# A two-layer graph kernel: the PSUM bank of three extra transposes, the queue of the last row's store, and the order of one step of layer 0

## The chip, the cores and the metric

The kernel runs on one core of a Trainium2 chip. The metric is the device time of one execution in microseconds (us). A core has TensorE (PE, matmuls and transposes; its weight loads are listed as PEld), VectorE (DVE), ScalarE (ACT), GpSimd (POOL) and SyncE (SP). DMAs are issued from the queues of SP, ACT and POOL. Matmul results land in PSUM banks, which are handed out here as named tiles with a number of buffers each.

## The reference, cut to what matters

There are N = 4096 nodes with 512 features, and an adjacency of 4096 x 4096 int32 in which about one entry in a thousand is 1. Two layers follow each other, each with a residual and a layer norm.

```python
# layer 0: graph attention, 8 heads of 64
Wh = einsum('nf,hfo->hno', x, W)
f1 = Wh . a[:, :64];  f2 = Wh . a[:, 64:]
e = leaky_relu(f1[:, :, None] + f2[:, None, :], 0.2)
e = where(adj > 0, e, -9e15)
x = layernorm(x + softmax(e) @ Wh)
# layer 1: mean of the neighbours
agg = (adj > 0) @ x / max(deg, 1)
out = concat([x @ W_self + b_self, agg @ W_nb + b_nb]) @ W_comb + b_comb
x = layernorm(x + relu(out))
```

## The kernel before, in words

The kernel never multiplies by the adjacency. It reads it once, turns each row into a short list of neighbours, and then gathers only the listed rows. Rows are handled in 32 blocks of 128 (`NB`). `FB` is 4, the number of 128-wide pieces of the 512 features. `LB` is 30 and `EARLY` is 29.

**Adjacency stage (lines 907 to 947).** Each step `b` of the loop issues on SP the load of an x block (`load_x`) and of an adjacency block (`load_adj`, two halves of 1 MB in four buffers `at`). It then works on four things:

- *Lists.* `some(lists)` moves a generator on by one piece. These pieces (`decode` and its callers) are VectorE work of many small instructions, with some PE work, and they turn keys into indices and weights for groups of four blocks.
- *Transposes.* `transposed(w + 1)` transposes an x block on PE (L320) into a PSUM tile `tp`, of which there is one buffer. ScalarE copies it to `xT`. The column sums of x are taken on VectorE in even blocks (L330) and with ScalarE's four copies in odd ones (L333); for blocks from 29 on it does the copy alone (L326). Their sums are taken earlier: steps 22, 23 and 24 transpose blocks 29, 30 and 31 a first time with `only=True`, and only VectorE's sum (L330) reads that result. These are the extra transposes.
- *Masks.* `key_bank(b + 1)` and `mask_adj(b + 1, h)` run on ScalarE; a mask (L395) turns half an adjacency block into bf16, in three buffers `ab`.
- *Node block.* `node_block(w, xT, b)` computes one block of Wh with its attention terms in two halves: `node_half` is four products in PSUM (L341, tile `pw`, two buffers) and a VectorE copy into `row` (L345). Between the halves PE folds the masks into keys (`fold_adj`, L413) and VectorE takes their maxima (`max_keys`, L428). `node_rest` has small copies on VectorE and GpSimd. The block's row is stored in the table `t0` in HBM from GpSimd's queue (`store`, L905).

**Between the stages (lines 938 to 987).** The last node block is computed and stored, the last masks and folds run, and two weights of 1 MB each are loaded from SP's queue (`load_fold`, L252 and L253). `gather(t0, ...)` on GpSimd then issues five indirect DMAs for a block (L590), which read rows of `t0`, so they wait for all rows to be stored. In the meantime the weights of layer 1 are multiplied out (`fold_weights`, L269 and L281) and the last lists are decoded.

**Layer 0 (lines 995 to 1054).** The loop over `i` runs from -2 to 32 and is a software pipeline: one step touches blocks `i - 1` to `i + 4`. On PE the order of a steady step is `a_reach` (L657), `a_z` of block `i - 1` (L721, four products of 512 columns with the folded weight), the transposes of block `i` (L320) with the copy to `xT` on ScalarE and its store on SP (L729), `a_shared_sum` of block `i + 2` (L638, two products of 8 columns) and `a_shared` of block `i + 1` (L684, two products of 512 columns, added to the x block that ScalarE put into the PSUM tile `nm`). VectorE's L700 adds `nm` to the gathered sum `y`, ScalarE's `root` and `norm` (L708 to L716) finish the layer norm, and L716 writes the block that the transposes read. In step 0 there is no `a_z` yet.

**What sets the order.** The order of the instructions on each engine is the order of the program (`tc.manual_schedule()`, L791). Nothing is reordered afterwards. Tiles come from pools by name, and a tile taken again waits until the last reader of the buffer is done; semaphores carry these waits. Each engine takes its instructions in order, and so each DMA queue's issues stand in the instruction order of the engine that issues them.

Of the kernel before, what the change touches and what calls it, by code (L numbers as in the profile page):

```python
# [31 lines left out]
F32 = mybir.dt.float32  # L32
# [8 lines left out]
P = 128  # L41
# [49 lines left out]
def listed_layers(  # L91
# [15 lines left out]
    nc = tc.nc  # L107
# [3 lines left out]
    FB = FIN // P  # L111
# [23 lines left out]
    ps = ctx.enter_context(tc.tile_pool(name="ps", bufs=1, space=PSUM))  # L135
# [179 lines left out]

    def transposed(b, wp, sums=None, only=False):

        tp = ps.tile([P, FB, P], F32, name="tp", bufs=1)
        for c in range(FB):
            nc.tensor.transpose(tp[:, c, :], xs[:, b, ts(c, P)], ident)  # L320
        if only:
            t = tp
        else:
            t = wp.tile([P, FB, P], F32, name="xT", bufs=2)
        if sums is None or b >= EARLY and not only:
            nc.scalar.copy(t, tp)  # L326
        elif only or b % 2 == 0:
            if not only:
                nc.scalar.copy(t, tp)
            nc.vector.tensor_reduce(sums[:, :, b : b + 1], tp, AX.X, OP.add)  # L330
        else:
            for c in range(FB):
                nc.scalar.activation(  # L333
                    t[:, c, :], tp[:, c, :], AF.Copy, accum_out=sums[:, c, b : b + 1]
                )
        return t

    def node_half(b, k, xT, w_sb, row):
        pw = ps.tile([P, HW], F32, name="pw", bufs=2)
        for c in range(FB):  # L340
            nc.tensor.matmul(  # L341
                pw, lhsT=xT[:, c, :], rhs=w_sb[:, c, k * HW : (k + 1) * HW],
                start=(c == 0), stop=(c == FB - 1),
            )
        nc.vector.tensor_copy(row[:, k * HW : (k + 1) * HW], pw)  # L345

    def node_rest(b, row):
        nc.vector.tensor_copy(lst[:, b, KL + 3 :], row[:, TW:FW])
        nc.vector.tensor_reduce(  # L349
            fmax[:, b, 0:1], row[:, 0:H], AX.X, OP.max, apply_absolute_value=True  # L350
        )
        nc.gpsimd.tensor_copy(  # L352
            f1s[:, b, 0:K0, :], lst[:, b, KL + 3 :].unsqueeze(1).to_broadcast([P, K0, H])
        )
# [29 lines left out]
    def load_adj(b, ap):  # L384

        for h in range(NH):
            at = loads[b, h] = ap.tile([P, NG // NH, SC], I32, name="at", bufs=4)
            r = b * P + h * (P // NH)
            nc.sync.dma_start(
                at, adj[r : r + P // NH, :].rearrange("(j r) (s c) -> (r s) j c", r=RG, s=SEG)  # L390
            )

    def mask_adj(b, h):
        ab = masks[b, h] = bp.tile([P, NG // NH, SC], BF16, name="ab", bufs=3)
        nc.scalar.activation(  # L395
            ab, loads.pop((b, h)), AF.Relu, accum_out=asum[:, b, h : h + 1]
        )
# [9 lines left out]
    def fold_adj(b, dp):  # L407

        key = keys[b]
        ab = [masks.pop((b, h)) for h in range(NH)]  # L410
        for k in range(0 if b in FIRST else 1, 3):
            for t in range(P // 32):
                nc.tensor.matmul(  # L413
                    key[ts(t, 32), :],
                    lhsT=two if k == 0 else fold[:, k - 1, :],
                    rhs=cols if k == 0 else ab[t // 2][:, 2 * (t % 2) + k - 1, :],
                    start=(k == 0), stop=(k == 2), tile_position=(0, 32 * t),
                    skip_group_check=b not in FIRST,
                )
        if b % G == 0:  # L420
            kks[b // G] = dp.tile([P, G, 3, NC], F32, name="kk", bufs=2)

    def max_keys(b):

        kk = kks[b // G][:, b % G, 0, :]
        key = keys.pop(b)
        for q in range(4):
            nc.vector.max(kk[:, q * 8 : (q + 1) * 8], key[:, ts(q, P)])  # L428
# [177 lines left out]
    def gather_early(b, pool):  # L606
        return gather(t1[0 : 2 + min(LE + b, LX) * P, :], b, pool, idxe)
# [26 lines left out]
    def a_shared_sum(b):  # L634

        DN[b] = ps.tile([P, H], F32, name="sm", bufs=2)
        for k in range(KH):
            nc.tensor.matmul(  # L638
                DN[b], lhsT=OWN[b][:, k, :], rhs=E[b][:, K0 + k, :],
                start=(k == 0), stop=(k == KH - 1),  # L640
            )
# [28 lines left out]
    def a_weigh(b, sl, to=None):  # L670
        gv = G0[b][:, sl, H:TW].rearrange("p k (h d) -> p k h d", h=H)
        nc.vector.tensor_tensor(  # L672
            gv if to is None else to.rearrange("p (k h d) -> p k h d", k=1, h=H), gv,
            E[b][:, sl].unsqueeze(3).to_broadcast([P, sl.stop - sl.start, H, D]), OP.mult,
        )
# [6 lines left out]
    def a_shared(b):  # L682
        for k in range(KH):
            nc.tensor.matmul(  # L684
                NM[b], lhsT=OWN[b][:, k, :], rhs=G0[b][:, K0 + k, H:TW],
                start=False, stop=(k == KH - 1), skip_group_check=True,
            )

    def a_adds(b, wp):

        yp = ps.tile([P, HD], F32, name="pw", bufs=2)
        a_weigh(b, slice(0, 1), yp)
        a_weigh(b, slice(1, K0))
        nc.vector.tensor_add(yp, yp, G0[b][:, 1, H:TW])
        Y[b] = wp.tile([P, HD], F32, name="y", bufs=2)
        nc.vector.tensor_add(Y[b], yp, G0[b][:, 2, H:TW])
# [106 lines left out]
    def weight(pool, name):  # L803
        return pool.tile([P, FB, HD], F32, name=name)
# [47 lines left out]
    xT = transposed(0, wp, sums)  # L852
# [27 lines left out]
    bcol = bias_columns(brw)  # L880


    def node_block(w, xT, between=None):
        row = wp.tile([P, FW], F32, name="row", bufs=2)
        node_half(w, 0, xT, w_sb, row)
        if between is not None:
            fold_adj(between, dp)
            max_keys(between)
        node_half(w, 1, xT, w_sb, row)
        node_rest(w, row)  # L890
        store(w, row, nc.gpsimd)
        return row

    def on_own(b):
# [9 lines left out]
    def store(w, row, eng=nc.scalar):  # L904
        eng.dma_start(t0[2 + w * P : 2 + (w + 1) * P, :], row[:, 0:TW])  # L905

    w, lists = 0, []
    for b in range(LB - 1):
# [7 lines left out]
        for k in range(1 + (b in AHEAD)):  # L916
# [8 lines left out]
            w, xT = w + 1, nxt  # L925
# [10 lines left out]
        if b % G == G - 1:  # L936
            lists = [decode(b + 1 - G, dp, on_own)]
    load_adj(LB + 1, ap)
    node_block(w, xT)
    key_bank(LB)  # L940
    mask_adj(LB, 0)
    m2 = weight(fp, "wr")
    loaded = load_fold(1, w_nb, m2, weight(fc, "wc"))
    fold_adj(LB - 1, dp)
# [45 lines left out]
    def on(b):  # L990
        return 0 <= b < NB
# [3 lines left out]
    for i in range(-2, NB + 1):  # L995
        if on(i):
            a_moments(i)
        if on(i - 1 + GA):
            G0[i - 1 + GA] = gather(t0, i - 1 + GA, gps[(i - 1 + GA) % GA])
        elif i > 0:  # L1000
            b = i - 1 + GA - NB
            G1[b] = gather_early(b, gps[(NB + b) % GA])
        if on(i + 1):
            a_reach(i + 1)
        if i == -1:
            for k in range(2):
                next(m2s)
        if i >= -1 and on(i + 2):
            a_owned(i + 2, wq)
        if on(i + 1):  # L1010
            a_x(i + 1)
            a_normed(i + 1)
            a_weigh(i + 1, slice(K0, KS))
        if on(i + 2):
            a_weights(i + 2, wq)
        if on(i):
            root(i, xs[:, i, :])
        if on(i + 2):
            a_exp(i + 2)
        for k in range({-2: 3}.get(i, 0)):  # L1020
            some(lists)
        if on(i):
            norm(i, xs[:, i, :])
        if on(i - 1):
            a_z(i - 1, XT.pop(i - 1), m2, wp)
        if on(i + 1):
            a_adds(i + 1, wq)
        if on(i):
            XT[i] = transposed(i, wp)
            store_xT(i, XT[i])  # L1030
        if on(i + 2):
            a_shared_sum(i + 2)
            for k in range({-2: 1}.get(i, 0)):
                some(lists)
            a_sum(i + 2, wq)
            for k in range({-2: 1}.get(i, 0)):
                some(lists)
        for k in range({-2: 3, -1: 2}.get(i, 0)):
            next(m2s)
        if on(i + 1):  # L1040
            a_shared(i + 1)
        if on(i + 3):
            a_owners(i + 3, wp)
        if 2 <= i < 6:
            next(biased)
        if i == 7:
            loaded = load_fold(0, w_self, m1, weight(fc, "wc"))
        if 16 <= i < 20:
            if i == 16:
                biased = fold_bias(loaded, bcol[:, 0:FB])  # L1050
            next(biased)
        if i == 20:
            sum_bias()
# [14 lines left out]
    xT = load_xT(0, wp)  # L1068
# [10 lines left out]
    for b in range(2):  # L1079
        nxt = load_xT(b + 1, wp)  # L1080
        g_self(b, xT, m1)
        xT = nxt
# [23 lines left out]
    for b in range(NB):  # L1106
# [5 lines left out]
        if b + 2 < NB:  # L1112
            nxt = load_xT(b + 3, wp) if b + 3 < NB else None
            g_self(b + 2, xT, m1)
            xT = nxt
# [413 lines left out]
```

## Time and profile before

| | us |
|---|---|
| three timed runs | 694.48, 692.57, 690.92 (median 692.57) |
| the profiled execution, its own time | 690.14 |
| its span, first to last instruction | 688.4 |
| PE busy | 622.5 (90%), 2354 instructions |
| VectorE busy | 499.1 (72%) |
| ScalarE busy | 456.0 (66%) |
| GpSimd busy | 348.8 (51%) |
| mean granted TensorE clock | 0.966 |

The span in stages, from PE's timeline: the adjacency loop runs to 225, the stage between to 264, and layer 0's loop with layer 1 behind it takes the rest. All starts that are named in this document are in us from the first instruction of the profiled execution.

To read the lines below: an instruction's line has its start, its duration, the engine, the line of the code, the operation, the tiles (output<-inputs), the shapes and the number of instructions in the row; in brackets stands the time that the engine stood idle just before, and what ended that wait. "issue" is time in which the engine waited for nothing that the profile shows. In the slices, each digit is the busy share of a fortieth of the span in tenths, and PEclk is the granted clock of TensorE in tenths of full speed.

### The profile page before, as it was taken

What the parts mean: (1) busy time and instruction counts of PE and PEld (TensorE: products, weight loads), DVE (VectorE), ACT (ScalarE), POOL (GpSimd) and SP (SyncE); (2) the same over time, 40 slices, a digit from 0 to 9 for tenths busy, and PEclk for the clock granted to TensorE, in tenths of its full rate; (3) what the DMA queues carried; (4) which work ended last, traced back from release to release, by engine and by line L of the source; (5) the groups of instructions that cost most, each with busy time, mean ns of one, the idle gap of its engine ahead of it and who ended that gap; (6) DMA issues with size and microseconds to landing.
All of it is one profiled execution on the core that took longest, in us unless ns stands there. A gap on an engine that the chain in (4) does not pass through costs nothing.

```text
span 688.4 us, 9188 instructions
## 1 busy us (share of the span) xinstructions
PE 622.5 (90%) x2354; PEld 344.6 (50%) x2354; DVE 499.1 (72%) x1431; ACT 456.0 (66%) x1044; POOL 348.8 (51%) x411
## 2 busy tenths in 40 slices
PE   4798988987799597999999999999899999999993
PEld 2466766665567354545455445454344444444441
DVE  6237987998598787999998998897304666666663
ACT  3687988878487534767676767776316567767764
POOL 4011111110001477777677776746676677777760
PEclk9989999999899698999999999999999999999997
DMA  8999999999799877989989888868878899998992
GB/s 249 405 408 408 409 408 409 407 409 407 262 321 354 298 193 213 281 277 277 379 275 290 260 275 259 279 209 281 271 210 278 283 297 311 317 308 299 323 306 76
DMA packets 91974, 209.65 MB, mean 305 GB/s; under 512 B 13694, under 2 KB 13702, under 8 KB 91914
## 3 DMA queue, kind: packets, MB, share of 16 engines
q1 hardware_dynamic: 63024, 114.05, 44.8%
q0 software_dynamic: 28704, 94.66, 44.1%
q8 instruction: 21, 0.34, 0.2%
q14 instruction: 39, 0.32, 0.2%
q10 hardware_dynamic: 186, 0.28, 0.1%
HBM read 175.25 MB, written 33.69 MB: 304 GB/s over the span
## 4 chain that ended last, share of the span: by engine, by line
PE 56%; DVE 4%; DMA 4%; POOL 3%; issue 3%; ACT 2%; SPq 0%; DVEq 0%; POOLq 0%; ACTq 0%
PE pw L721 13%; PE nm L753 8%; PE pw L753 8%; PE nm L684 7%; PE nm L760 4%; PE pw L760 4%; POOL g L590 3%; PE tp L281 2%; PE tp L320 2%; PE pw L341 2%; PE sm L657 2%; DMA wc<-in_L_gnn_W_comb_dram 2%; PE sm L638 1%; DMA g<-t,idx 1%; DMA t<-row 1%
## 5 line engine op out<-in xcount | busy, mean ns | idle before, releaser
L590 POOL DMA_INDIRECT g<-t,idx x290 | 280.3, 967 | 109.1 <-issue 49.7
L395 ACT ACTIVATE ab<-at 128x2048 bf16<-128x2048 int32 x64 | 122.3, 1912 | 41.0 <-DMA at<-in_adj_dram 27.8
L341 PE MATMUL pw<-w_sb,xT 128*128 128x264 f32 x512 | 134.4, 409 | 7.0 <-issue 3.8
L721 PE MATMUL pw<-wr,xT 128*128 128x512 f32 x256 | 117.7, 603 | 0.7 <-ACT xT L326 0.7
L341 PEld LDWEIGHTS pw<-w_sb,xT 128*128 128x128 f32 x512 | 97.1, 199 | 36.0 <-issue 7.7
L352 POOL COPY f1s<-lst 128x24 f32<-128x24 f32 x32 | 7.8, 245 | 183.1 <-DVE fmax L349 100.5
L672 DVE TENSOR_TENSOR g<-g,key 128x1024 f32<-128x1024 f32 x64 | 77.9, 1217 | 1.1
L721 PEld LDWEIGHTS pw<-wr,xT 128*128 128x128 f32 x256 | 46.3, 191 | 47.2 <-issue 46.3
L684 PE MATMUL nm<-g,own 128*128 128x512 f32 x128 | 64.5, 627 | 0.0
L320 PE MATMUL tp<-ident,xs 128*128 128x128 f32 x268 | 44.9, 293 | 18.3 <-DVE sums L330 12.1
L753 PE MATMUL pw<-m,xT 128*128 128x512 f32 x128 | 57.6, 592 | 0.0
L753 PE MATMUL nm<-m,xT 128*128 128x512 f32 x128 | 57.6, 592 | 0.0
L320 PEld LDWEIGHTS tp<-ident,xs 128*128 128x128 f32 x268 | 32.3, 150 | 46.7 <-ACT xs L716 21.7
L707 ACT ACTIVATE xs<-y,ln_sum 128x512 f32<-128x512 f32 x32 | 23.1, 723 | 42.2 <-DVE y L700 40.2
L776 DVE SCALAR_TENSOR_TENSOR sm<-y,lst,nm 128x512 f32<-128x512 f32 x16 | 12.1, 756 | 52.9 <-PE nm L770 29.1
L345 DVE COPY row<-pw 128x264 f32<-128x264 f32 x64 | 26.9, 424 | 23.0 <-PE pw L341 17.4
L753 PEld LDWEIGHTS pw<-m,xT 128*128 128x128 f32 x128 | 24.4, 190 | 30.6 <-issue 30.3
L753 PEld LDWEIGHTS nm<-m,xT 128*128 128x128 f32 x128 | 24.4, 190 | 30.6 <-issue 30.6
L590 POOL DMA_INDIRECT g<-t,idxe x30 | 28.4, 947 | 18.2 <-issue 5.5
L281 PE MATMUL tp<-wc,row 128*128 128x512 f32 x64 | 30.9, 622 | 2.0 <-ACT m L285 1.2
L760 PE MATMUL nm<-g,own 128*128 128x512 f32 x64 | 30.2, 594 | 1.2 <-ACT nm L744 1.2
L684 PEld LDWEIGHTS nm<-g,own 128*128 128x128 f32 x128 | 22.5, 196 | 16.3 <-issue 15.6
(210 smaller groups left out, 1068.3 us busy)
## 6 DMA issues: line engine op xcount, KB each, us to landing
at<-in_adj_dram SPq DMA_DIRECT2D x64, 1024.0 KB, 10.7
t<-row POOLq DMA_DIRECT2D x32, 260.0 KB, 5.5
xt<-xT SPq DMA_DIRECT2D x32, 256.0 KB, 4.0
t<-row SPq DMA_DIRECT2D x32, 256.0 KB, 4.2
xT<-xt SPq DMA_DIRECT2D x32, 256.0 KB, 5.4
out_dram<-row SPq DMA_DIRECT2D x32, 256.0 KB, 5.2
xs<-in_x_dram SPq DMA_DIRECT2D x31, 256.0 KB, 10.9
g<-t,idx POOLq DMA_INDIRECT x290, 4.9
```

The source lines that it names most:

```text
L281: nc.tensor.matmul(mp, lhsT=wT[:, d, :], rhs=wc[:, d, :], start=(d == 0), stop=(d == FB - 1))
L320: nc.tensor.transpose(tp[:, c, :], xs[:, b, ts(c, P)], ident)
L341: nc.tensor.matmul(pw, lhsT=xT[:, c, :], rhs=w_sb[:, c, k * HW : (k + 1) * HW], start=(c == 0), stop=(c == FB - 1),)
L345: nc.vector.tensor_copy(row[:, k * HW : (k + 1) * HW], pw)
L395: nc.scalar.activation(ab, loads.pop((b, h)), AF.Relu, accum_out=asum[:, b, h : h + 1])
L590: nc.gpsimd.indirect_dma_start(out=out, out_offset=None, in_=table, in_offset=bass.IndirectOffsetOnAxis(ap=at, axis=0),)
L672: nc.vector.tensor_tensor(gv if to is None else to.rearrange("p (k h d) -> p k h d", k=1, h=H), gv, E[b][:, sl].unsqueeze(3).to_broadcast( ...
L684: nc.tensor.matmul(NM[b], lhsT=OWN[b][:, k, :], rhs=G0[b][:, K0 + k, H:TW], start=False, stop=(k == KH - 1), skip_group_check=True,)
L707: nc.scalar.activation(wide, Y[b], AF.Square, bias=MV[b], scale=-float(HD), accum_out=rs)
L721: nc.tensor.matmul(pz, lhsT=xT[:, c, :], rhs=m2[:, c, :], start=(c == 0), stop=(c == FB - 1))
L753: nc.tensor.matmul(NM[b], lhsT=xT[:, c, :], rhs=m1[:, c, :], start=False, stop=(c == FB - 1), skip_group_check=True,)
L760: nc.tensor.matmul(NM[b], lhsT=OWN[b][:, k, :], rhs=g[:, K0 + k, 0:HD], start=False, stop=(k == KH - 1), skip_group_check=True,)
```

## The change

Three edits are made together.

1. The extra transposes of steps 22 to 24 (`only=True`) are written to a buffer of the tile `pw`, the two banks that the halves of the node block use in turn. Before, they were written to the one bank `tp`, which all other transposes use.
2. The row of the last node block in the adjacency stage isn't stored from GpSimd's queue at the end of `node_block`. It is stored from ScalarE's queue, which issues it after `key_bank(LB)` and `mask_adj(LB, 0)`.
3. In step 0 of layer 0, `a_shared_sum(2)` and `a_shared(1)` are issued ahead of the transposes of block 0 and of what belongs to them (the copy to `xT`, and its store). In all other steps the order stays.

```diff
     def transposed(b, wp, sums=None, only=False):
 
-        tp = ps.tile([P, FB, P], F32, name="tp", bufs=1)
+        tp = ps.tile(
+            [P, FB, P], F32, name="pw" if only else "tp", bufs=2 if only else 1
+        )
...
-    def node_block(w, xT, between=None):
+    def node_block(w, xT, between=None, keep=False):
...
         node_rest(w, row)
-        store(w, row, nc.gpsimd)
+        if not keep:
+            store(w, row, nc.gpsimd)
         return row
...
     load_adj(LB + 1, ap)
-    node_block(w, xT)
+    row = node_block(w, xT, keep=True)
     key_bank(LB)
     mask_adj(LB, 0)
+    store(w, row)
     m2 = weight(fp, "wr")
...
         if on(i + 1):
             a_adds(i + 1, wq)
+        if i == 0:
+            a_shared_sum(i + 2)
+            a_shared(i + 1)
         if on(i):
             XT[i] = transposed(i, wp)
             store_xT(i, XT[i])
         if on(i + 2):
-            a_shared_sum(i + 2)
+            if i:
+                a_shared_sum(i + 2)
...
-        if on(i + 1):
+        if on(i + 1) and i:
             a_shared(i + 1)
```

`store` itself is unchanged. Its default queue is ScalarE's:

```python
    def store(w, row, eng=nc.scalar):
        eng.dma_start(t0[2 + w * P : 2 + (w + 1) * P, :], row[:, 0:TW])
```

## The prediction

> **What bounds the kernel now.** I read four views in this order: the slices of the span, to find a stage in which every engine is low at once; the timelines of the stage found, engine by engine; the chain of work that ended last, to see who sets the pace behind it; and the waits of the few lines that the edits touch.
>
> ```profile
> PE   4798988987799597999999999999899999999993
> ACT  3687988878487534767676767776316567767764
> PEclk9989999999899698999999999999999999999997
> DMA  8999999999799877989989888868878899998992
> ```
>
> A slice is 17.2 us. Slices 0 to 9 are the adjacency stage at its best: DMA at 9 and 408 GB/s. In slice 10 (172 to 189 us) PE falls to 7, ScalarE to 4 and DMA to 7, although adjacency rows are still to come. Asked by stretches, 175 to 185 us has PE busy 5.20 of 10 us at a clock of 0.66, and 185 to 195 us moves 141 GB/s. Nothing is the bound there: something waits. PE's timeline names it:
>
> ```profile
> 168.45 1.11 PE L320 MATMUL tp<-ident,xs 128*128 128x128 f32 x4 [1.23 <-ACT xT L333]
> ...
> 174.60 0.64 PE L320 MATMUL tp<-ident,xs 128*128 128x128 f32 x4
> 180.03 1.11 PE L320 MATMUL tp<-ident,xs 128*128 128x128 f32 x4 [4.80 <-DVE sums L330]
> 180.94 3.72 PE L341 MATMUL pw<-w_sb,xT 128*128 128x264 f32 x8
> 184.60 0.71 PE L413 MATMUL nm<-ab,fold 128*32 128x512 bf16 x8
> 185.23 2.05 PE L341 MATMUL pw<-w_sb,xT 128*128 128x264 f32 x8
> ...
> 190.69 0.66 PE L320 MATMUL tp<-ident,xs 128*128 128x128 f32 x4 [1.23 <-ACT xT L333]
> ```
>
> The second set of transposes in each of steps 22, 23 and 24 (168.45, 180.03, 190.69) is the extra one. It waits 1.23, 4.80 and 1.23 us for the one bank `tp`, since the first set must be read out of it. In step 23 that reader is VectorE:
>
> ```profile
> 179.29 0.68 DVE L330 TENSOR_REDUCE sums<-tp 128x4 f32<-128x512 f32 x1
> 181.18 0.69 DVE L330 TENSOR_REDUCE sums<-tp 128x4 f32<-128x512 f32 x1 [1.21 <-PE tp L320]
> ```
>
> VectorE reaches that sum only at 179.29, behind list work. Behind the stalled transposes on PE stand both Wh halves and the fold of step 23 (184.60), whose reading frees a mask buffer, so ScalarE stands too:
>
> ```profile
> 176.27 1.91 ACT L395 ACTIVATE ab<-at 128x2048 bf16<-128x2048 int32 x1
> ...
> 185.40 1.91 ACT L395 ACTIVATE ab<-at 128x2048 bf16<-128x2048 int32 x1 [7.12 <-issue]
> 224.85 1.91 ACT L395 ACTIVATE ab<-at 128x2048 bf16<-128x2048 int32 x1 [1.15 <-issue]
> ```
>
> After that PE sets the pace: 195 to 225 us has PE busy 29.91 of 30 us, and the chain runs through PE from there, then over masks, gathers and VectorE's decoding to layer 0, and through PE (L721, L684, L753, L760) to the end. So time saved before 195 us stays saved if nothing else comes late.
>
> **What the Trainium skill says.** "PSUM — Partial Sum Buffer", section "PSUM bank collisions raise a hardware error", asks for a semaphore guard by bank: a second writer of `tp` waits for the reader of all of it; the 4.80 us agree. Its section "Engine vs sequencer instructions" calls the queues of ScalarE, VectorE and GpSimdE strict FIFO: what stands behind a waiting issue waits too. "TensorE: Matmul & The Clock Gate", part 1, says that the clock is halved after an idle free-running window of about 3.4 us. The trace agrees, and is finer: asked window by window, PE busy 0.63 of 3.41 us (174.60 on) and 1.29 (263.35 on) are followed by a clock of 0.50; 1.68 (92.68 on) and 1.84 (51.72 on) aren't. "DMA: Bandwidth & Descriptors", section "Specifications", gives first bytes after about 1 us from GpSimd and 0.6 us from SP or ScalarE; here a 260 KB store from POOL lands after 5.5 us in the median, a 256 KB store from SP after 4.2.
>
> **The change, part by part.** All starts are of this execution.
>
> *Extra transposes in `pw`.* Three sets move, none is added: 4 x 0.13 us each. `pw` has two banks in rotation, so extra, half 0, half 1 now take three turns. The wait moves: half 1 takes the bank of the extra set and waits for its sum.
> Step 22: extra at 167.05; half 0 needs VectorE's copy of the half before (167.56 + 0.42), so 168.05 in place of 169.36. At half clock till 171.18 it ends at 171.5, where the fold now starts at 172.14: 0.64 us earlier. Half 1 needs the extra sum (170.37 + 0.66): no wait; 172.05 in place of 172.69.
> Step 23: VectorE copies half 1 at 174.0 to 174.43. First transposes 174.05, extra 174.55, half 0 at 175.05 (1.88 us), fold to 177.5. VectorE's list work between is unchanged: L478, at 175.39 now, to the sum at 179.29 is 3.90 us, so from 174.62 the sum is at 178.52, and the extra sum follows at once, to 179.80. Half 1 starts at 179.87 in place of 185.23: 5.36 us earlier, behind a new wait of 2.37 us. The mask at 185.40 moves to about 177.7.
> Step 24: the eight L493 products at 181.75, VectorE's L499 at 183.5 (now 189.02), and 4.48 us of its work later (189.02 to 193.50) the extra sum, 187.98 to 188.65. Half 1 at 188.7 in place of 193.60: **4.9 us earlier**, new wait 1.8 us. From here PE has no wait to 224, and I carry 4.9 us. DMA allows it: the load issued at 187.42 now goes out near 179.7 and, at 10.7 us to landing, is there at 190.4; its mask is at 199.03 - 4.9 = 194.1.
> The unknown is the clock: the new wait leaves PE busy about 1.55 us in the window from 178.01, between the 1.29 that halved it and the 1.68 that didn't. If it is halved, one window costs about 1.85 us. I take no halving and keep -3.05 as the other end.
>
> *Last Wh row from ScalarE.* POOL loses one issue (0.55 us). ScalarE gains one, between the masks that start at 221.71 and 224.85. It waits for the row's copy (DVE L345 at 224.26, 0.43), so until about 224.75; the three small stores of L246 to L248 took 0.24 to 0.28 us on ScalarE's queue, the x load 0.36. The mask behind it starts at 225.1 instead of 224.85; ScalarE then has no gap to 231.1, PE's last fold and VectorE's L428 at 232.36 wait for it: **+0.25 us**. The gathers gain but don't need it:
>
> ```profile
> 225.20 0.55 POOL L905 DMA_DIRECT2D t<-row  x1
> 232.54 1.05 POOL L590 DMA_INDIRECT g<-t,idx  x1 [6.79 <-PE sm L477]
> ```
>
> The releaser named isn't the cause: POOL's own wait before the first gather lasts 6.14 us from 225.3, and the store of 225.20 lands after 6.2. From ScalarE it lands 4.2 to 6.2 us after 224.75, so gathers start 0 to 2.5 us earlier, my value 2. But the first row's five gathers (fifth at 237.92) have landed by 242.7, at 4.8 us at most, and their first user is VectorE L628 at 250.84, which comes straight from list work. The cover is 8 us; the gain is 0, and a store landing up to 8 us late costs nothing either.
>
> *Shared product first in step 0.* Two L638 products and two L684 (eight passes) move ahead of four transposes on PE; the copy to xT and the store to xt (SP, empty then) move with them.
>
> ```profile
> 268.05 1.12 PE L320 MATMUL tp<-ident,xs 128*128 128x128 f32 x4 [3.41 <-ACT xs L716]
> 268.96 0.86 PE L638 MATMUL sm<-e,own 128*128 128x8 f32 x4
> 269.67 3.76 PE L684 MATMUL nm<-g,own 128*128 128x512 f32 x4
> ```
> ```profile
> 273.47 0.69 DVE L700 SCALAR_TENSOR_TENSOR y<-y,nm 128x512 f32<-128x512 f32 x1 [2.67 <-PE nm L684]
> ```
>
> L638 needs ScalarE's exp (267.06 + 0.24): 267.35. L684 then runs 268.0 to 271.7, VectorE's L700 1.75 us earlier, but the transposes end at 272.8 instead of 269.2. ScalarE is in order: the xT copy, owners, st and nm stand ahead of the next L707, which so starts at about 274.4, now 274.20. Its norm ends 2.93 us later, and PE's next transposes, at 277.28 now, don't move: **0**. If the shorter pause (2.7 us for 3.41) leaves the clock up, L684 takes 1.9 us, and the next transposes come at 274.9: -2.4 us. If the pause falls worse in its windows, I allow +1.
>
> Sum: -4.9 + 0.25 + 0 = -4.65 us on the profiled execution: 690.14 to 685.5 (its span is 688.4, 1.7 us lie around it). The three timed runs have a median of 692.57, 2.4 above it; the same difference on that gives **687.9**.
>
> **Rivals.**
> A, as worked out: 687.9, chance 0.42.
> B, the clock is halved in the new wait: -3.05 + 0.25 gives 689.8. For it: 1.55 us is nearer to unknown than to safe. 0.25.
> C, A and a full clock in step 0: 687.9 - 2.4 = 685.5. Against it: a pause of 2.7 us can still fill most of one window. 0.13.
> D, the bank change only renames the wait: if VectorE reaches the extra sum of step 23 near 185, half 1 stands as long as now, and 692.6 + 0.25 = 692.8. Against it: the sum waited 1.21 us for PE itself at 181.18, so it isn't VectorE that was late. 0.12.
> E, slower: the issue on ScalarE is held while the loads before it drain. Issues of x rows on SP, each behind two adjacency loads, took 0.33 to 5.04 us, 1.14 in the median; here 2 MB of weights are ahead, issued at 221.73 and 222.28, the second landing 13.0 us later, at 235.3. A hold until then, 10.5 us from 224.75, keeps the masks behind it: 692.6 - 4.9 + 10.5 = 698.2. It decides from a hold of 4.9 us. Against it: 0.24 us at 47 us, with DMA as full. 0.08.
>
> **How the numbers follow.** About 0.5%, 3.5 us, is what a measurement of this kernel can tell from no change: below 689.1 is faster, above 696.0 slower. The timed runs spread by 1.9 us around their median. Faster: 0.36 of A's 0.42, 0.09 of B, all of C: 0.58. Slower: most of E and, with the phase of the clock, a little of D; I give 0.07. Same: 0.35. The range goes from a little below C, 684.8, to D's middle, 692.5; outside lie E, half of D and the tail of C, under 0.2.
>
> **What would show it.** Right: no wait ahead of the extra transposes; waits near 2.4 and 1.8 us ahead of half 1 in steps 23 and 24, ended by the sums; no gap of 7 us on ScalarE; the fold of step 23 near 177, all PE starts around 200 to 220 near 4.9 us earlier; the store issue on ScalarE below 0.4 us; the first user of gathers without a wait for DMA; in step 0, L700 earlier but the next transposes not. Wrong: half 1 waiting 5 us or more; a clock of 0.50 in 181 to 185; a mask held by the store; a shift before 195 us that is gone by 225, which would mean that loads or masks, not PE, pace that stage.

## The result, and the profile after

The changed kernel takes 691.70 us in the median of 20 runs (688.04 to 694.32), the kernel before 692.85 us in the median of 20 (689.15 to 696.40). The ratio is 0.9973, with a 95% interval from 0.9956 to 0.9990: 1.9 us faster, with 0.7 and 3.0 us as ends (the two medians lie 1.15 us apart). The forecast was 4.65 us. In the runs below, all but those of first_4, bank_3, bank_sm_2 and sm_warm_2, every kernel, before among them, took 785 to 810 us in the median, because VectorE and ScalarE paused again and again behind 240 us, mostly for 7 to 15 us and for a reason that isn't known; of those runs only the stretch up to 222 us is read, and a median only beside that of before from the same group.

The profiled execution of the changed kernel has a time of 692.97 us and a span of 691.2, so it is longer than the profiled execution of before (688.4), although the median is shorter. A pair of single profiles can't give the verdict here; they show where time moves. The slices of the changed kernel:

```profile
PE   4688998897798698999999999999899999999993
ACT  3677988888777434667677767776316567767764
PEclk9999999999999587999999999999999999999997
DMA  8999999999899877788989888968978889998991
```

The hole in slice 10 (ScalarE 4, PE 7, DMA 7 in before) is gone: ScalarE 7, DMA 8. In slices 13 to 15, from 225 us on, PEclk has 5, 8 and 7, where before has 6, 9 and 8; that is read further down. PE's timeline of steps 23 and 24 in the changed kernel (lines behind the first edit have numbers higher by 2 and more, so L320 is L322, L330 is L332, L341 is L343):

```profile
173.63 0.63 PE L322 MATMUL tp<-ident,xs 128*128 128x128 f32 x4
174.10 0.60 PE L322 MATMUL pw<-ident,xs 128*128 128x128 f32 x4
...
176.41 0.61 PE L415 MATMUL nm<-ab,fold 128*32 128x512 bf16 x8
179.66 2.05 PE L343 MATMUL pw<-w_sb,xT 128*128 128x264 f32 x8 [2.63 <-DVE sums L332]
...
186.03 0.62 PE L415 MATMUL key<-ab,fold 128*32 128x512 bf16 x8
188.66 3.67 PE L343 MATMUL pw<-w_sb,xT 128*128 128x264 f32 x8 [2.02 <-DVE sums L332]
```

The extra set at 174.10 no longer waits. Half 1 does, for 2.63 us in step 23 and 2.02 us in step 24, each time for VectorE's sum. And half 1 of step 24 takes 3.67 us where 2.05 is its time at full clock. Asked window by window, in the grid on which the clock changes (columns: PE busy, PEld, DVE, ACT, POOL, granted clock, DMA share, GB/s):

```profile
core 0: us, PE busy (x) PEld busy (x) DVE busy (x) ACT busy (x) POOL busy (x), PEclk, DMA share, GB/s
174.91:178.33 3.42, 2.11 (x16) 1.11 (x14) 3.17 (x9) 3.42 (x4) 0.36 (x1) 1.00 1.05 375
178.33:181.74 3.41, 2.08 (x11) 1.83 (x11) 2.40 (x8) 2.07 (x6) 0.00 (x0) 1.00 1.05 408
181.74:185.15 3.41, 3.41 (x28) 3.28 (x28) 2.24 (x11) 1.23 (x9) 0.74 (x2) 1.00 1.05 396
185.15:188.57 3.42, 1.49 (x13) 0.59 (x11) 3.25 (x9) 3.42 (x4) 0.00 (x0) 1.00 0.31 122
188.57:191.98 3.41, 3.32 (x8) 2.60 (x9) 1.18 (x6) 0.79 (x2) 0.00 (x0) 0.50 0.93 309
```

The wait of step 24 leaves PE busy 1.49 us in the window from 185.15, and the next one has half the clock. The wait of step 23 is divided between two windows (2.11 and 2.08 us busy) and costs no clock.

To follow the time, the starts of the same instruction are subtracted. Two instructions of VectorE's list work frame steps 22 to 24: a MAX8 (L456) and a reduction (L515). VectorE's timeline has them in before and, below, in the changed kernel:

```profile
168.16 0.25 DVE L456 MAX8 nb<-kj 128x8 f32<-128x96 f32 x1
...
215.07 0.26 DVE L515 TENSOR_REDUCE jx<-jk 128x8 f32<-128x104 f32 x1
```
```profile
167.62 0.25 DVE L458 MAX8 nb<-kj 128x8 f32<-128x96 f32 x1
...
211.76 0.26 DVE L517 TENSOR_REDUCE jx<-jk 128x8 f32<-128x104 f32 x1
```

The first comes 0.54 us earlier than in before, the second 3.31 us earlier. So these steps gained **2.77 us** in this execution. Below, "gain" is this difference for each kernel, and "shift" is how much later or earlier (minus) an instruction starts than in before's profile.

### The profile page after: what moved, and what is told of

Its sections match the earlier page's. It is cut to its first block, busy times and chain, and to the rows that moved or that the text cites. A ratio compares the mean times of both kernels' runs of the same rounds, so it can differ in the third digit from the quotient of the medians.

```text
span 691.2 us, 9191 instructions
## 1 busy us (share of the span) xinstructions
PE 626.3 (91%) x2354; PEld 345.0 (50%) x2354; DVE 498.4 (72%) x1431; ACT 455.6 (66%) x1044; POOL 348.0 (50%) x410
## 3 DMA queue, kind: packets, MB, share of 16 engines
HBM read 175.25 MB, written 33.69 MB: 302 GB/s over the span
## 4 chain that ended last, share of the span: by engine, by line
PE 60%; DVE 14%; DMA 14%; ACT 4%; issue 4%; POOL 2%; SPq 1%; DVEq 0%; ACTq 0%; POOLq 0%
PE pw L723 12%; DMA at<-in_adj_dram 11%; PE nm L755 8%; PE pw L755 8%; PE nm L686 7%; PE pw L343 5%; PE nm L762 4%; PE pw L762 4%; PE tp L281 3%; ACT ab L397 3%; POOL g L592 2%; PE tp L322 2%; PE sm L659 2%; DMA g<-t,idx 2%; PE sm L640 1%
## 5 line engine op out<-in xcount | busy, mean ns | idle before, releaser
L343 PE MATMUL pw<-w_sb,xT 128*128 128x264 f32 x512 | 133.3, 407 | 10.7 <-DVE sums L332 4.7
L723 PE MATMUL pw<-wr,xT 128*128 128x512 f32 x256 | 119.7, 611 | 1.4 <-ACT xT L328 1.3
L343 PEld LDWEIGHTS pw<-w_sb,xT 128*128 128x128 f32 x512 | 96.2, 197 | 39.6 <-issue 7.3
L723 PEld LDWEIGHTS pw<-wr,xT 128*128 128x128 f32 x256 | 47.0, 194 | 49.3 <-issue 47.5
L686 PE MATMUL nm<-g,own 128*128 128x512 f32 x128 | 64.5, 627 | 0.0
L322 PEld LDWEIGHTS tp<-ident,xs 128*128 128x128 f32 x256 | 30.2, 147 | 36.3 <-ACT xs L718 18.4
L322 PE MATMUL tp<-ident,xs 128*128 128x128 f32 x256 | 41.7, 287 | 7.4 <-DVE sums L332 7.1
L281 PE MATMUL tp<-wc,row 128*128 128x512 f32 x64 | 34.1, 676 | 2.0 <-ACT m L285 1.2
L686 PEld LDWEIGHTS nm<-g,own 128*128 128x128 f32 x128 | 22.5, 196 | 16.3 <-issue 15.9
```

The lines of the kernel that those rows point to most:

```text
L281: nc.tensor.matmul(mp, lhsT=wT[:, d, :], rhs=wc[:, d, :], start=(d == 0), stop=(d == FB - 1))
L343: nc.tensor.matmul(pw, lhsT=xT[:, c, :], rhs=w_sb[:, c, k * HW : (k + 1) * HW], start=(c == 0), stop=(c == FB - 1),)
L686: nc.tensor.matmul(NM[b], lhsT=OWN[b][:, k, :], rhs=G0[b][:, K0 + k, H:TW], start=False, stop=(k == KH - 1), skip_group_check=True,)
L723: nc.tensor.matmul(pz, lhsT=xT[:, c, :], rhs=m2[:, c, :], start=(c == 0), stop=(c == FB - 1))
```

## The experiments

Edit 1 alone, edit 2 alone, edit 3 alone, and edits 1 and 2 are the hunks of the change that the front of this document shows, the others left out.

> Only edit 1, the extra transposes in the bank of the Wh halves. In the profile after, the shift against before grew from -0.54 us at 166 us to -3.31 at 215, so edit 1 gave 2.77 there with the clock halved once in a new wait. Theory T (edit 1 gives its 2.8 us, and what was missing in the end came from half-clock windows between 226 and 280 whose place changes with every run, and a little from edit 2): 2.8 us faster in the timed runs, with an interval of about 1.2 either way, and a shift of -2.5 to -5 at 215. Rival R1 (the stage between absorbs the gain, because VectorE's list work or the gathers set the time there): 1 us faster or less, with the shift at 215 as above and gone by 262 although the half-clock windows are the same in number.

> Only edit 2, the last row stored from ScalarE. In the profile after, ScalarE had no mask between 220.29 and 221.88, where it waited for the row's copy, and the shift went from -3.31 to -2.66 between 215 and 232. Theory T: slower by 0.2 to 0.7 us, not told from 0 by the timed runs; the mask after the store starts 0.2 to 0.4 us later than in before, and the first user of the gathers doesn't move earlier. Rival R2 (the earlier gathers give something): 0.5 to 2 us faster, with the first use of gathers earlier by as much.

> Only edit 3, the shared product ahead of the transposes in step 0 of layer 0. Theory T (PE's order in that step doesn't decide, the granted clock does): within 0.6 us of before in the timed runs; in the profile the next transposes of step 1 come within 0.5 us of before if the half-clock windows of the step are the same. Rival R3 (the transposes, their copy and ScalarE's later work really come later, so step 0 loses what edit 1 gained): 1.3 to 1.7 us slower, with VectorE's list of step 1 and all behind it shifted by as much.

> Edits 1 and 2 without edit 3. Theory T: 2.3 us faster than before, that is within 0.7 of edit 1 alone and 0 to 1 us faster than all three edits. Rival R3 (edit 3 costs 1.3 to 1.7 us): 3 to 3.5 us faster than before. Rival R1 (the gain is absorbed between the stages): 1 us faster or less.

> Only edit 1 once more, since in the first call the stages behind 250 us took over 100 us longer for every kernel, before among them. What the first call did show: from 166 to 215 us the three executions with edit 1 gained 2.77, 3.87 and 1.79 us, and three with the old bank 0.00, 1.40 and -0.13. Theory T: 2.4 us faster than before, give or take 1.2. Rival R1 (absorbed between the stages): 1 us faster or less.

> Only edit 3 once more, for the same reason. Theory T: within 0.6 us of before. Rival R3 (the transposes of step 0 and what follows really come later): 1.3 to 1.7 us slower.

> Only edit 3, a third time; in the two calls so far gathers and the load of the second weight came so late for every kernel that step 0 couldn't be read. Theory T: within 0.6 us of before, and step 1's transposes within 0.5 us of before's where the half-clock windows are the same. Rival R3: 1.3 to 1.7 us slower. If gathers are late again, only the stages up to 225 us can be read, where this kernel is the kernel before.

> Only edit 3, once more, for step 0 of layer 0, which the calls so far didn't let read (pauses of VectorE and ScalarE of 7 to 15 us fell there in every kernel). In the profile after, step 0 lost 1.68 us against before, and with it a third half-clock window from 273.90, which follows a window with the four transposes and short products that edit 3 put behind the shared product. Theory T (edit 3 by itself moves nothing but can add a half-clock window): between 0.5 us faster and 1.7 us slower, from 0 to 1.7 us in step 0 according to the window. Rival R3 (always 1.3 to 1.7 us slower).

> Only edit 1, timed in the state in which the result was measured. Theory T: 2.6 us faster than before, give or take 0.9, so 0.7 us or less from all three edits together (1.9 us). Rival R7 (edits 2 and 3 take more than the 0.34 us seen on the mask): 3.5 us or more faster than before.

What the profiles and the times gave, together with the kernels described further down (bank_fill was run once, every other kernel 6 times or more):

| kernel | bank of the extra set | gain, us | half-clock windows from 163 us to the reduction | median, us (before beside it) |
|---|---|---|---|---|
| before | tp | 0 | 3 | 692.85 |
| only_store | tp | 1.39 | 2 | 807.35 (808.59) |
| only_first | tp | -0.13 | 3 | 805.24 (808.59) |
| first_2 | tp | 1.23 | 2 | 798.66 (807.62) |
| first_3 | tp | -0.24 | 3 | 798.10 (798.80) |
| first_4 | tp | -0.49 | 3 | 692.82 (692.14) |
| after | pw | 2.77 | 2 | 691.70 (692.85) |
| only_bank | pw | 3.87 | 1 | 804.72 (808.59) |
| bank_and_store | pw | 1.79 | 3 | 802.10 (808.59) |
| bank_2 | pw | 3.87 | 1 | 804.17 (807.62) |
| warm_gap | pw | 3.86 | 1 | 803.90 (807.62) |
| bank_3 | pw | 3.86 | 1 | 690.78 (692.34) |
| bank_fill | pw, wait filled | 4.40 | 1, in step 22 | 789.88 (800.94) |
| act_sums | pw, sums on ScalarE | 4.87 | 1 | 801.60 (807.62) |
| bank_nm, nm_warm | nm | 9.94, 9.96 | 0 | 791.38, 787.49 (798.80) |
| bank_sm, sm_warm | sm | 9.95, 9.95 | 0 | 785.46, 790.07 (800.94) |
| bank_sm_2 | sm | 9.97 | 0 | 684.75 (692.14) |
| sm_warm_2 | sm | 9.96 | 0 | 681.13 (692.34) |

*Edit 1.* The six executions with the pw bank gain 2.77, 3.87, 1.79, 3.87, 3.86 and 3.86, in the mean 3.34 us; the six with tp (before's own 0 among them) 0.29. The difference is **3.04 us**, not 4.9. It goes with the half-clock windows: with pw 3.87, 2.77 and 1.79 for one, two and three of them, about 1.0 us each. With tp three windows give -0.49 to 0, two give 1.23 and 1.39. So at the same number of windows pw is 1.5 to 2.0 us better in the mean, and the rest of the 3.04 is that it had fewer of them. By time, bank_3 has a ratio of 0.9977 (0.9956 to 0.9998), which is 1.6 us, with ends at 0.1 and 3.0. The expectation of 2.6 lies inside; so does R1's 1 us, which the time alone doesn't exclude (for R1 see "Behind 222 us"). Rival R7 isn't borne out: edit 1 alone isn't seen to be faster than all three edits (1.9 us).

*Edit 2.* Shown by ScalarE's timeline of the changed kernel, around the store (ACTq is its queue):

```profile
221.41 0.35 ACTq L908 DMA_DIRECT2D t<-row  x1
221.88 1.91 ACT L397 ACTIVATE ab<-at 128x2048 bf16<-128x2048 int32 x1 [1.50 <-DVE lst L350]
```

The mask stands 1.50 us where it stood 1.15, and the shift goes from -3.31 to -2.97 at this mask. It is 0.34 or 0.35 us in only_store and bank_and_store too, and 0.00 in only_bank, bank_2 and first_4. The issue takes 0.35 us and isn't held. R2's gain from earlier gathers isn't there: in the changed kernel their first user (L630, at 249.45) starts behind list work, after 0.20 us of idle time that no DMA ended.

*Edit 3.* The ratio of first_4 is 1.0000 (0.9975 to 1.0025). R3's 1.3 to 1.7 us would be 1.0019 to 1.0025, at the upper edge, so the profile has to decide. Step 0 in first_4, which has two half-clock windows there as before has:

```profile
271.68 1.02 PE L638 MATMUL sm<-e,own 128*128 128x8 f32 x4 [2.71 <-ACT e L632]
272.56 3.76 PE L684 MATMUL nm<-g,own 128*128 128x512 f32 x4
276.11 1.06 PE L320 MATMUL tp<-ident,xs 128*128 128x128 f32 x4
...
281.52 0.66 PE L320 MATMUL tp<-ident,xs 128*128 128x128 f32 x4
```

All of first_4 is 4.32 us later than before when step 0 begins, and step 1's transposes (281.52 against 277.28) come 4.24 later: -0.08 us from the edit. So R3, which says always 1.3 to 1.7 us, falls. In the changed kernel there is a third window at half clock:

```profile
core 0: us, PE busy (x) PEld busy (x) DVE busy (x) ACT busy (x) POOL busy (x), PEclk, DMA share, GB/s
263.66:267.07 3.41, 0.88 (x6) 0.56 (x4) 2.66 (x8) 2.36 (x9) 2.63 (x3) 1.00 0.78 226
267.07:270.49 3.42, 3.25 (x7) 2.03 (x8) 3.22 (x6) 0.82 (x2) 2.51 (x4) 0.50 0.77 213
270.49:273.90 3.41, 3.39 (x11) 2.34 (x10) 1.45 (x6) 1.13 (x4) 2.50 (x4) 0.50 0.77 215
273.90:277.31 3.41, 3.41 (x5) 1.33 (x5) 3.34 (x6) 3.03 (x10) 1.83 (x2) 0.50 0.78 248
```
```profile
271.67 1.06 PE L322 MATMUL tp<-ident,xs 128*128 128x128 f32 x4
272.52 0.86 PE L659 MATMUL sm<-dn,st 128*128 128x8 f32 x4
273.41 5.62 PE L723 MATMUL pw<-wr,xT 128*128 128x512 f32 x8
278.87 0.60 PE L322 MATMUL tp<-ident,xs 128*128 128x128 f32 x4
```

L723 takes 5.62 us for 3.68, and step 1's transposes come 1.69 us later than the shift of -0.10 ahead of step 0 gives. The window before, from 270.49, looks full (3.39 us), but after 271.9 it holds the transposes, the 8-column products and 0.5 us of L723. It holds 1.4 us of L686. In first_4 the window from 274.23 holds 2.1 us of L684 and is followed by the full clock. So edit 3 cost 0 us in one execution and 1.7 us in another, and the 1.7 is the third window. That the windows' place decides it is likely, but two executions don't show it.

*The wait filled.* In edit 1's kernel, between the fold and half 1 of steps 23 and 24, eight transposes into an sm bank that nobody reads:

```diff
+    def warm(n):
+        tp = ps.tile([P, FB, P], F32, name="sm", bufs=2)
+        for c in range(n):
+            nc.tensor.transpose(tp[:, c % FB, :], xs[:, 0, ts(c % FB, P)], ident)
...
             max_keys(between)
+            if between in (23, 24):
+                warm(8)
         node_half(w, 1, xT, w_sb, row)
```

> Edit 1 (pw), and eight transposes that nobody reads, about 1 us, in the waits of 2.63 and 2.02 us ahead of half 1 in steps 23 and 24. This tests the term of the sum that was left at nothing: the half clock in the new wait. Theory T (the waits halve the clock and that took away half of the gain): no half-clock window between 172 and 222, the two waits shorter by about 1 us with half 1 not later than with edit 1 alone, and a shift from 166 to 215 of -4.7 to -5.5 us, against -3.2 in the mean of five executions with edit 1 and -4.9 in the prediction's working at a full clock. Rival R6 (the clock isn't it; the working's 4.9 was itself too much): shift of -3.9 at most, with no half window.

```profile
177.31 1.09 PE L343 MATMUL sm<-ident,xs 128*128 128x128 f32 x8
180.02 2.05 PE L348 MATMUL pw<-w_sb,xT 128*128 128x264 f32 x8 [1.61 <-DVE sums L332]
...
186.94 1.09 PE L343 MATMUL sm<-ident,xs 128*128 128x128 f32 x8
189.03 2.05 PE L348 MATMUL pw<-w_sb,xT 128*128 128x264 f32 x8 [1.00 <-DVE sums L332]
```

No half clock behind either wait, and a gain of 4.40 us, although one window at half clock (168.20) remains in step 22, as in before's profile. The changed kernel has that window too (168.09), and then the one from 188.57: its gain is 1.63 us smaller, and its half 1 of step 24 took 1.62 us longer (3.67 for 2.05). So the half clock behind the wait is what the filling took away. The 4.40 lies between T's 4.7 and R6's 3.9: the clock takes most of what is missing from 4.9, and the working was too large by some 0.5. This is one execution.

*The sums on ScalarE.* Edit 1, and the sum of the extra set as in odd rows:

```diff
         if only:
-            t = tp
+            for c in range(FB):
+                nc.scalar.activation(
+                    junk, tp[:, c, :], AF.Copy, accum_out=sums[:, c, b : b + 1]
+                )
+            return None
...
+    junk = xa.tile([P, P], F32, name="junk")
```

> Edit 1, and the sums of the three extra sets on ScalarE (four accumulating copies of 0.28 us each, as in odd rows) in place of VectorE, where they stood behind list work. Theory T (the new wait ahead of half 1 is VectorE's list work, and the half clock comes from that wait): no wait over 0.6 us ahead of half 1 in steps 23 and 24, no half-clock window between 178 and 222, a shift of -6 to -9 us at 215, and 5 to 8 us faster than before in the timed runs. Rival R4 (adjacency loads or the list work itself pace these steps): the waits only move to other instructions, shift at 215 of -2 to -4.5.

A miss. The waits stay, with another end, the copy of half 0 (L349), which stands behind the same list work on VectorE:

```profile
178.40 2.05 PE L345 MATMUL pw<-w_sb,xT 128*128 128x264 f32 x8 [2.38 <-DVE row L349]
...
187.15 3.48 PE L345 MATMUL pw<-w_sb,xT 128*128 128x264 f32 x8 [1.76 <-DVE row L349]
```

The gain is 4.87 and not 6 to 9. The wait moved, as R4 says, though the gain is above R4's 4.5. ScalarE is done with the extra set of step 23 at 175.96, so why half 1 then stands until VectorE's copy is done (178.34) isn't shown. To take the sum from VectorE isn't enough; next another bank was tried.

*Another bank.* Edit 1 alone with another name in place of pw:

```diff
-            [P, FB, P], F32, name="pw" if only else "tp", bufs=2 if only else 1
+            [P, FB, P], F32, name="sm" if only else "tp", bufs=2 if only else 1
```

and the same with "nm". With nm the keys of the steps behind come out otherwise, so its lists, and the rows that it gathers, aren't the reference's; the instructions are the same. (The Trainium skill, "Advanced Engine Details and Errata", section "PSUM Accumulation (`has_written` bits)", says that the first matmul of a group clears the marks of its bank, and that a later accumulating write then overwrites. That would explain it, since the folds of the keys accumulate onto what ScalarE wrote; no run here shows it.)

> The extra transposes in the two banks of the tile nm (keys of odd steps) in place of pw, all else as before. In steps 22 to 24 at least one nm bank is free, so neither the next transposes nor half 1 should wait for VectorE's list work. Theory T (what held TensorE, before and with edit 1, is a bank whose reader stands behind the list work, and the clock is halved by that wait): no wait over 0.6 us on TensorE between 171 and 222, no half-clock window there, a shift from 166 to 215 of -6 to -8.5 us against -3.2 in the mean of five executions with edit 1; 4 to 8 us faster than before in the timed runs. Rival R4 (the list work or the adjacency loads pace these steps themselves): the waits move to the 128x24 products, to masks or to the half copies, and the shift stays between -2 and -5.

> The extra transposes in the two banks of the tile sm (otherwise used by the short products of the list work) in place of pw. With the nm banks the shift from 166 to 215 was -9.94 us with no wait and no half-clock window, but there the keys of the steps behind were changed, so that kernel computed other lists than the reference's; here nothing of the computation is changed. Theory T: the same: no wait over 1 us on TensorE between 167 and 222, no half-clock window there, a shift of -9 to -10.5 us, and 6 to 10 us faster than before in the timed runs. Rival R4 (sm is claimed by the list work's own short products, so the wait comes back on them): shift between -2 and -7.

> The sm banks once more, beside before on this chip. Theory T: a shift of -9 to -10.5 us from 166 to 215 and 6 to 10 us faster in the timed runs; where the pauses after 230 us are again there, up to 16.

Steps 23 and 24 in bank_sm_2:

```profile
174.70 0.61 PE L415 MATMUL nm<-ab,fold 128*32 128x512 bf16 x8
175.25 2.05 PE L343 MATMUL pw<-w_sb,xT 128*128 128x264 f32 x8
177.13 1.86 PE L495 MATMUL sm<-lst,own 128*128 128x24 f32 x16
...
182.16 2.05 PE L343 MATMUL pw<-w_sb,xT 128*128 128x264 f32 x8
184.05 0.60 PE L322 MATMUL tp<-ident,xs 128*128 128x128 f32 x4
185.16 2.05 PE L343 MATMUL pw<-w_sb,xT 128*128 128x264 f32 x8 [0.51 <-DVE row L347]
```

VectorE's two instructions in bank_sm_2:

```profile
168.25 0.25 DVE L458 MAX8 nb<-kj 128x8 f32<-128x96 f32 x1
...
205.19 0.26 DVE L517 TENSOR_REDUCE jx<-jk 128x8 f32<-128x104 f32 x1
```

No wait ahead of either half 1 (175.25 and 182.16), no half clock between the two instructions, and 9.94 to 9.97 us in all six executions with nm or sm. Half 0 and half 1 keep the two pw banks to themselves, and from 167 to 185 us PE doesn't wait for VectorE once. The ratio of bank_sm_2 is 0.9869 (0.9837 to 0.9902): 9.1 us faster, with ends at 6.8 and 11.3. R4 falls for this bank: neither the loads nor the list work pace these steps.

*The clock behind the loop.* Transposes that nobody reads, in PE's waits, added to edit 1 (warm_gap) and to the nm and sm banks (nm_warm, sm_warm). Here `warm` writes to a pw bank, and ahead of step 0 to tp:

```diff
     key_bank(LB + 1)
+    warm(8)
     fold_adj(LB, dp)
...
         some(lists)
+    warm(8)
     fold_adj(LB + 1, dp)
...
     for k in range(7):
         some(lists)
+        if k == 1:
+            warm(8)
...
+        if i == 0:
+            warm(12, "tp")
         if on(i):
             XT[i] = transposed(i, wp)
```

> Edit 1, and extra transposes that nobody reads (eight, about 1 us, ahead of each of the last two folds and ahead of the following 128x24 products; twelve ahead of step 0's transposes) in the time in which TensorE waits. Theory T (half-clock windows after 226 eat the gain): of the 7 to 9 windows at half clock from 224 to 276 at most 3 are left, and it is 3 to 6 us faster than edit 1 alone. Rival R5 (TensorE isn't the bound there, so its clock costs little): fewer windows, but within 1 us of edit 1 alone.

> As the kernel with the nm banks, and with the extra transposes that nobody reads in TensorE's waits from 221 to 235 and ahead of step 0 of layer 0. Theory T: at most 3 half-clock windows after 220 up to step 2 of layer 0, against 6 to 9 in before and after; 2 to 5 us faster than with the nm banks alone. Rival R5 (TensorE's clock costs little there, since VectorE or a DMA comes later): within 1 us of the nm banks alone.

> The sm banks, and the extra transposes that nobody reads in TensorE's waits from 212 to 226 and ahead of step 0 of layer 0. Theory T: 1 to 4 us faster than with the sm banks alone, from fewer half-clock windows up to step 2 of layer 0. Rival R5 (TensorE's clock costs little there): within 1 us.

> The sm banks and the transposes that nobody reads in TensorE's waits behind the adjacency loop and ahead of step 0, in the state in which the result was measured. Theory T: 1 to 4 us faster than the sm banks alone (9 us faster than before), with at most 4 half-clock windows from 212 to 270 against 7 to 9. Rival R5 (TensorE's clock costs little there): within 1 us of the sm banks alone.

sm_warm_2 has a ratio of 0.9834 (0.9789 to 0.9879), 11.5 us faster than before, and four half-clock windows from 212 to 270 against eight in bank_sm_2. By the means, 8.6 and 11.1 us, it is 2.5 us better than bank_sm_2, with an error of about 1.5; sm_warm's median is 4.6 us above bank_sm's. So the total isn't settled, but step 0 can be read: with the clock kept up, L691 (L684 in before) takes 1.96 us for 3.76, and VectorE's L700 comes 2.56 us earlier than the shift ahead of it gives.

```profile
255.87 1.51 PE L343 MATMUL tp<-ident,xs 128*128 128x128 f32 x12
259.42 0.66 PE L322 MATMUL tp<-ident,xs 128*128 128x128 f32 x4 [2.04 <-ACT xs L723]
259.91 0.51 PE L645 MATMUL sm<-e,own 128*128 128x8 f32 x4
260.28 1.96 PE L691 MATMUL nm<-g,own 128*128 128x512 f32 x4
```

nm_warm and warm_gap have no total that can be read. bank_sm_2 and sm_warm_2 are both faster than before; neither was timed beside the changed kernel.

*Behind 222 us.* The shift in the profiles that have no pauses, at the last mask (229.18 in before) and at PE's last product ahead of step 0 (L657, 264.14 in before), with the half-clock windows between the loop and that product:

| kernel | shift at the reduction | at the last mask | at 264.14 | half-clock windows |
|---|---|---|---|---|
| before | 0 | 0 | 0 | 4 |
| sm_warm_2 | -10.31 | -8.56 | -8.63 | 4 |
| bank_3 | -4.10 | -4.11 | -2.19 | 6 |
| first_4 | 0.48 | 2.47 | 4.32 | 6 |
| bank_sm_2 | -9.88 | -8.36 | -5.84 | 6 |
| after | -3.31 | -2.72 | -0.10 | 6 |

From the last mask to 264.14 nothing is lost with four windows, and 1.9 to 2.6 us with six. bank_3 loses 1.92 there and first_4, with before's bank, 1.85: at the same number of windows R1's absorption isn't seen. So the changed kernel's own profile has lost all but 0.10 us of its gain by step 0, mostly through products that ran at half clock (before first, the changed kernel below):

```profile
241.02 4.51 PE L281 MATMUL tp<-wc,row 128*128 128x512 f32 x8
254.44 2.82 PE L281 MATMUL tp<-wc,row 128*128 128x512 f32 x6
```
```profile
238.37 5.99 PE L281 MATMUL tp<-wc,row 128*128 128x512 f32 x8
253.05 4.52 PE L281 MATMUL tp<-wc,row 128*128 128x512 f32 x6
```

Ahead of that, up to 2 us go at the last mask where its adjacency load comes late: in first_4 ScalarE waits 1.89 us for it, in before's profile not at all.

## Why the prediction was wrong, step by step

- *What bounds the kernel* was read rightly. The 4.80 us were a bank wait behind VectorE's list work, and what is saved in steps 22 to 24 is still there at 215 us (3.31) and, less edit 2's 0.34, at 222 us. "So time saved before 195 us stays saved if nothing else comes late" holds behind that only where the windows of the clock are the same (the table above).
- *The moves of edit 1* came near to what was worked. Half 1 of step 23 was put at 179.87 with a wait of 2.37: 179.66 and 2.63. Half 1 of step 24 at 188.7 with 1.8: 188.66 and 2.02. The mask at 177.7: 177.20. Of the 4.9 us, 0.54 came from this execution's earlier start into step 22, so the worked gain was too large by as much; bank_fill's 4.40 agrees. With these 0.54 us taken out, half 1 comes later than worked by 0.2 us in step 22, 0.33 in step 23 and 0.5 in step 24. The first 0.2 is the fold of step 22, which was taken at its full-clock time and took 0.89 us at half clock.
- *The clock is the step that failed*: "I take no halving and keep -3.05 as the other end." The new waits were priced with nothing for the clock, and in none of the six executions with the pw bank did both pass without a half-clock window behind them. The prediction asked for one phase of the windows (where they begin), before's, and for one wait, step 23's. There it would have been right in the changed kernel (2.08 us busy); the halving came behind step 24's wait, which it hadn't tested, and in the four kernels with one window in this stretch behind step 23's; bank_and_store has one behind each. With every execution the grid lies elsewhere (its windows begin at 178.01 us in before, 178.33 in the changed kernel, 179.09 in bank_3). The Trainium skill, "TensorE: Matmul & The Clock Gate", part 1, says of the start of a kernel that the windows' phase differs when the same kernel is measured again ("it's run-variable"); the traces agree for its middle, and the prediction, which cites that part, didn't use it. Half 1 of step 24 lost 1.62 us (3.67 for 2.05), where the prediction priced a window at 1.85. Rival B, at 0.25, was the case; A, at 0.42, needed two waits of 2 us or more to miss the grid. That B's 3.05 is so near to the difference of the means (3.04) is luck: it is 4.9 less one window of 1.85, and the means hold executions with one to three windows; against before's profile the changed kernel shows 4.40 less 1.62.
- *Edit 2* was right in kind: +0.25 worked, 0.34 measured, because ScalarE waited for the row. No hold, so E falls. First gathers at 228.65, 0.9 us earlier than the shift at the masks (2 worked), and the first user starts without a wait for a DMA: nothing gained. (That it "comes straight from list work" in before is not quite so: its line there has 0.21 us of idle time ended by a gather.)
- *Edit 3*: 0 worked, -0.08 measured in first_4. The +1 that was allowed for a worse fall of the windows was 1.7 in the changed kernel. The -2.4 for a full clock is -2.44 in sm_warm_2 (step 1's transposes at 266.21 for 277.28, with -8.63 ahead), but transposes that nobody reads got it, not the order.
- *The sum* in B's form is 3.04 - 0.34 = 2.7 us; measured are 1.9 (0.7 to 3.0), and 1.6 for edit 1 alone. The difference is within the error of the runs. Before's own profiled execution, 2.7 us under its median, was a lucky one to add moves to: it has four half-clock windows ahead of step 0, where first_4, with the same code there, has six, and no wait for the last adjacency load. Whether the saved time changes where these windows fall, in the mean, stays open.

## What to carry to other kernels

Giving a stalled write a bank from a tile that is busy itself moves the wait to that tile's next user; look for a bank whose next user isn't held up by that, since here pw gave 3 us and sm 10. A wait that is shortened but not removed is priced with the clock that it may cost, over all phases of the windows and for each such wait, not for the phase of one profile. A gain of a few us is read from the stretch it belongs to, in several executions, and then checked in the median of many runs.

## What the runs showed of the hardware

Over the 20 profiles, from 30 us on, 3667 full-clock windows of 3.41 us were counted by PE's busy time. After less than 1.3 us the next window was at half clock in 239 of 239 cases; from 1.3 to 1.5 in 27 of 35, from 1.5 to 1.7 in 12 of 34, from 1.7 to 2.1 in 10 of 60, from 2.1 to 2.7 in 7 of 298, and above that in 8 of 3001. A window already at half clock was followed by another in all 240 cases with less than 2.7 us busy, and in 35 of 51 from 2.7 to 3.0: to get the clock back took about twice the busy time that was enough to keep it, so one short wait can cost several windows. Busy time isn't all of it: the windows from 250.01 and 270.49 of the changed kernel were busy 3.18 and 3.39 us, the first with products of 8 and 24 columns in it, the second with 8-column products and 128-column transposes, and were still followed by half the clock (the second was at half clock itself). bank_3, bank_sm_2 and first_4 have a window like the first at the same place in the code: busy 3.10, 3.14 and 2.98 us, with half the clock behind it.
